# A gated-recurrence and mixture-of-experts layer on one core: the router in four column tiles, normalised rows turned by VectorE by way of DRAM, and the first expert's rows gathered whole

## The chip, the cores and the metric

The kernel runs on one core of a Trainium2 chip. The metric is the device time of one execution in microseconds; the time before is the median of three runs. A profile of one further execution goes with it. All arithmetic is in float32.

## The reference, cut to what matters

The input is 8 sequences of 1024 tokens with 512 features, 8192 tokens in all. Every token's row is normalised, and the normalised row feeds two branches whose product is added to the input.

```python
xn = layernorm(x)                                # (8192, 512)
# branch 1: a gated recurrence over each sequence
hidden, forget, inp = split(xn @ W1 + b1, 3)     # three times 1024 features
s = scan_over_time(hidden, forget, inp, init_h) @ W2 + b2
# branch 2: a shared expert, and one of 32 routed experts per token
shared = (silu(xn @ sgate) * (xn @ sup)) @ sdown # 1024 wide
logits = xn @ gate_w                             # (8192, 32)
e, top = argmax(logits), max(logits)
xs = xn * sigmoid(top)
routed = (silu(xs @ rgate[e]) * (xs @ rup[e])) @ rdown[e]
out = x + s * silu(shared + routed)
```

## The kernel before, in words

**Dense stage.** The tokens go in 16 chunks of 512, each of four tiles of 128 rows. For a chunk the kernel needs the normalised rows transposed: `xnT`, features on the partitions in four blocks k. From it come the recurrence's three projections and the shared expert's gate and up projections, as 20 jobs of 256 output features. The weights of a job are loaded as `nat`. From chunk 1 on, a job is done as Strassen's seven products (P1 to P7, L638), with sums of weight blocks (`sums`, kept in DRAM, L544) and differences of `xnT` blocks (`t`, "t sums", L570). ScalarE evicts each product, and VectorE or GpSimd joins them in pairs (L664); the tiles for P1's eviction, tag `p1`, have two buffers. Beside the jobs run the cell and gate arithmetic (reciprocal, sigmoid, scan, L702 to L784) and the second projections, the "fill" (L925), whose weights `wP` are fetched as each unit ends (L855, L858).

**The order.** In this stage the order of instructions is written out by hand. Time is counted in slots; a chunk has 140 of them (SC), and in each slot one product of two matmuls is issued. From chunk 1 on a slot lasts about 1.22 us. `at(slot, step)` places a step in a slot; each engine then does its instructions in the order in which they were issued, and waits for what they need. After the last chunk the slots go on with fill alone. Sync (SP) issues the plain DMAs and GpSimd (POOL) the indirect ones, each in its own order.

**Preparation of the next chunk.** `Prep.plan` places, in the slots of chunk c, what chunk c+1 needs (50 slots later in chunk 0): load of the rows, statistics, the power that gives 1/sigma (`spread`, on POOL), `normal` (L392), `transpose` on TensorE through PSUM with an eviction by ScalarE (L405, L408), the router's matmuls (L416), a transposition of the logits back to token rows (L426), the argmax (`choose`, L436 to L444), the score, and `scale`, which multiplies the normalised rows by the score and stores them to `rec1` (L453, L454). `rec2` holds x, the recurrence's output and the shared expert's output, for the experts' last step. The tiles x, `lgT` and the larger tiles of the table share a pool of five buffers.

**The table of tokens by expert.** `Dispatch` counts, for every token, its rank in its expert (`ranks`, every four chunks; two matmuls `bef`, L1000 and L1003, that need the running sums L989), then sorts the experts by size (`places`), gives each token a cell (`slots`), and writes token numbers by 64 scatters on POOL (`enter`, L1172) into eight tables, which are read back (`collect`) and merged (`merge`). `idx` holds the merged token numbers, and `fours` numbers of quarter rows, made from a copy of the table in DRAM (`numbers`, L1207). Numbers become available only at the passage to the experts.

**The experts.** Each of the 32 chunks has a fixed width, 376 tokens at most. `gather_in` (L199) fetches `xs` in pieces: each indirect DMA brings quarter rows of 32 tokens, so that VectorE's transposition of 32 by 32 blocks (L222) gives features on partitions. `gather_rest` (L210) fetches the rows of `rec2`; a VectorE addition (L272) waits for it. Then `compute` does gate, up and down products (L247, L236) with `h` from VectorE between (L255). In this stage the framework orders the instructions.

Of the kernel before, what the change touches and what calls it, by code (L numbers as in the profile page):

```python
# [33 lines left out]
def tile_kernel(  # L34
# [39 lines left out]

    nc = tc.nc
    B, S, H = x.shape
    N = B * S
# [86 lines left out]
    class Chunk:  # L166
# [3 lines left out]

        def __init__(self, alloc, alloc_w, name, cols, fours, width, w_src):
# [20 lines left out]
        def gather_in(self):  # L194
            self.xs = []
            for t, n in self.tiles:
                r = self.alloc([P, NA, HA], "xs", f"{self.name}_xs{t}")
                for b in range(-(-n // BL)):
                    nc.gpsimd.indirect_dma_start(  # L199
                        out=r[:, b, :], out_offset=None,  # L200
                        in_=rec1.rearrange("n (a d) -> (n a) d", a=NA),
                        in_offset=bass.IndirectOffsetOnAxis(ap=self.fours(t, b), axis=0),
                    )
                self.xs.append(r)

        def gather_rest(self):
            self.rest = []
# [8 lines left out]
        def transpose(self, t):  # L216
            if t >= len(self.tiles):
                return
            nb = -(-self.tiles[t][1] // BL)
            if t == 0:  # L220
                self.xsT = self.alloc([P, KH, C], "xsT", f"{self.name}_xsT")
            nc.vector.transpose(  # L222
                self.xsT[:, :, t * P : t * P + nb * BL].rearrange("p k (b c) -> p b k c", c=BL),
                self.xs[t][:, :nb, :].rearrange("p b (r k) -> p b k r", k=KH),
            )
# [72 lines left out]
    def alloc2(shape, tag, name):  # L298
# [3 lines left out]

    chunks = [
        Chunk(
            alloc2, alloc_w, f"e{e}", 
            lambda t, e=e: pools["idx"][:, e * CT + t : e * CT + t + 1],
            lambda t, b, e=e: pools["fours"][:, b, e * CT + t : e * CT + t + 1],
            WIDTHS[e], lambda e=e: expert(eid[0:1, e : e + 1]),
        )
        for e in range(E)  # L310
    ]
# [44 lines left out]
    class Prep:  # L356
# [37 lines left out]
                ALU.subtract, ALU.mult,  # L394
            )

        def transpose(self, t):
            if t == 0:
                xnTs[self.c] = jp.tile([P, KH, T], FP, tag="xnT", name=f"xnT{self.c}")
            if self.c or t > 1:  # L400
                tp = work(f"tp{self.c * NT + t}")
            else:
                tp = ps_x.tile([P, 512], FP, tag=f"x{t}", name=f"tp{t}")
            for k in range(KH):
                nc.tensor.transpose(  # L405
                    tp[:, k * P : (k + 1) * P], self.xs[t][:, k * P : (k + 1) * P], ident
                )
            nc.scalar.copy(  # L408
                xnTs[self.c][:, :, t * P : (t + 1) * P],
                tp.rearrange("p (k q) -> p k q", k=KH),  # L410
            )

        def router(self):
            lgp = work(f"lgp{self.c}")
            for k in range(KH):
                nc.tensor.matmul(  # L416
                    lgp[:E, :], lhsT=gw[:, k, :], rhs=xnTs[self.c][:, k, :],
                    start=(k == 0), stop=(k == KH - 1),
                )
            self.lgT = xp.tile([E, T], FP, tag="x", name=f"lgT{self.c}")  # L420
            nc.scalar.copy(self.lgT, lgp[:E, :])

        def logits(self):
            self.ps = work(f"lgt{self.c}")
            for t in range(NT):
                nc.tensor.transpose(  # L426
                    self.ps[:, t * E : (t + 1) * E], self.lgT[:, t * P : (t + 1) * P],
                    ident[:E, :E],
                )

        def choose(self):

            c = self.c
            lg = self.ps[:, : NT * E].rearrange("p (t e) -> p t e", t=NT)
# [60 lines left out]
    nc.sync.dma_start(out=gw, in_=gate_w.rearrange("(k p) e -> p k e", p=P))  # L495

    def zero_rows():
        for a in range(NA):
# [457 lines left out]
    class Dispatch:  # L956
# [16 lines left out]
        def ranks(self, q):  # L973
# [22 lines left out]
            yield  # L996
            yield
            yield
# [11 lines left out]
            )  # L1010
            yield
            nc.vector.tensor_reduce(rank[:, q : q + G], prev, AX.X, ALU.add)
            yield
            if q + G == NTILE:
                self.totals = work("cps")
                nc.tensor.matmul(
# [171 lines left out]
        def merge(self, which):  # L1188
            two = self.two
            if which < 2:  # L1190
                nc.vector.tensor_tensor(two[which], two[which], two[which + 2], ALU.min)
            elif which == 2:
                nc.vector.tensor_tensor(two[0], two[0], two[1], ALU.min)
            else:
                nc.vector.tensor_tensor(two[0][:, 0, :], two[0][:, 0, :], two[0][:, 1, :], ALU.min)
                self.table = dram.tile([P, NCOL], FP, name="table")
                nc.sync.dma_start(out=self.table[:, :], in_=two[0][:, 0, :])

        def numbers(self, half):

            if half == 0:
                nc.vector.tensor_copy(pools["idx"], self.two[0][:, 0, :])
# [47 lines left out]
    def spread_out(gen):  # L1250
        if next(gen, gen) is not gen:
            at(now + 1, spread_out, gen)

    at(SC + 90, d.clear)
    for q in range(NCHUNK // GC - 1):
        at(SC * (GC * (q + 1) - 2) + 80, lambda q=q: spread_out(d.ranks(q)))
    last = SC * (NCHUNK - 1)

    def table():
        for part in (d.ranks(NCHUNK // GC - 1), d.places(), d.slots()):  # L1260
            yield from part
        first = max(now + 3, last - 2)
        end = first + (12 * NTILE) // 5
        for i in range(NTILE):
            at(first + (12 * i) // 5, d.enter, i)
        at(end + 4, d.collect)
        for which in range(4):
            at(end + 13 + which, d.merge, which)
        for half in range(2):
            at(max(end + 20, END + 1) + half, d.numbers, half)  # L1270
# [159 lines left out]
```

## Time and profile before

| what | us |
|---|---|
| median of three runs | 4409.75 |
| lowest and highest | 4408.37, 4411.7 |
| the profiled execution | 4412.07 |
| its span, first to last instruction | 4410.3 |
| dense stage up to the last chunk's first product | 2654 |
| first product of the first expert, at | 2899 |

In the profile, PE is TensorE's matmuls and PEld its weight loads, DVE is VectorE, ACT is ScalarE, POOL is GpSimd, and SP is Sync; a q behind an engine's name is its queue of DMA issues. A row of groups gives line, engine, operation, output and inputs, shapes and count, then busy time and mean ns of one, then the idle time of the engine just before them, and who ended it. A row in order of time gives start, length, engine and line, and in brackets the wait ahead of it. A float32 matmul is two matmul instructions. A PE record runs to the end of its pipeline, so what a matmul costs TensorE is read from one start to the next.

### The profile page before, as it was taken

How to read it: one execution, taken by the hardware profiler on the slowest of the kernel's cores; microseconds unless marked ns; L12 is line 12 of the kernel's file. 1: busy time of each engine (PE TensorE's matmuls, PEld its weight loads, DVE VectorE, ACT ScalarE, POOL GpSimd, SP SyncE). 2: the span in 40 equal slices, each digit the busy share in tenths (PEclk: the TensorE clock that was granted, in tenths of full speed). 3: DMA queues.
4: the chain of work that ended last, by engine and by line, in shares of the span. 5: the costliest groups of instructions: out<-in, count | busy, mean ns of one | idle time of the engine just before them, and what ended most of it. 6: DMA issues, size and time to landing. Idle time of an engine off the chain costs nothing. (4 is left out here: it accounts for less than half of the span.)

```text
span 4410.3 us, 52402 instructions
## 1 busy us (share of the span) xinstructions
PE 4317.4 (98%) x19259; PEld 3586.4 (81%) x19259; DVE 2729.3 (62%) x3431; ACT 1709.4 (39%) x3379; POOL 1773.1 (40%) x1419
## 2 busy tenths in 40 slices
PE   8899999999999999999999999979999999999998
PEld 3488888888888888888888888846777788889997
DVE  6776876786977767877777698713333434443332
ACT  3355555555555555555555554401111111111111
POOL 4445343444444435444534456642233323332210
PEclk9999999999999999999999999989999999999999
DMA  7555655556556565555565555555455556565661
GB/s 239 186 185 185 202 186 196 179 196 208 177 188 204 187 195 184 193 202 177 195 202 188 194 172 177 179 202 177 174 195 209 181 180 226 183 236 197 216 227 63
DMA packets 408121, 842.39 MB, mean 191 GB/s; under 512 B 30060, under 2 KB 249868, under 8 KB 399669
## 3 DMA queue, kind: packets, MB, share of 16 engines
q1 hardware_dynamic: 380132, 749.01, 50.1%
q0 software_dynamic: 27728, 89.99, 6.4%
q8 instruction: 154, 2.52, 0.2%
q14 instruction: 107, 0.87, 0.1%
HBM read 756.20 MB, written 100.77 MB: 194 GB/s over the span
## 5 line engine op out<-in xcount | busy, mean ns | idle before, releaser
L638 PE MATMUL b<-t,sums 128*128 128x256 f32 x2400 | 617.1, 380 | 5.5 <-DVE t L570 3.9
L925 PE MATMUL u<-wP,s 128*128 128x256 f32 x2048 | 601.1, 380 | 2.7 <-DMA wP<-tdram 1.9
L236 PE MATMUL e_acc<-e_h,e_wd 128*128 128x296 f32 (+15 forms) x2048 | 515.4, 397 | 17.6 <-DVE e_h L255 17.5
L247 PE MATMUL e_g<-e_xsT,e_wg 128*128 128x296 f32 (+15 forms) x2048 | 520.4, 397 | 9.6 <-DVE e_xsT L222 8.2
L247 PE MATMUL e_u<-e_xsT,e_wu 128*128 128x296 f32 (+15 forms) x2048 | 518.0, 396 | 0.0
L638 PEld LDWEIGHTS b<-t,sums 128*128 128x128 f32 x2400 | 456.2, 190 | 70.7 <-issue 6.0
L199 POOL DMA_INDIRECT e_xs<-rec,fours x288 | 273.3, 949 | 561.2 <-DVE e_xsT L222 467.0
L236 PEld LDWEIGHTS e_acc<-e_h,e_wd 128*128 128x128 f32 x2048 | 389.9, 191 | 106.7 <-DVE e_h L255 19.1
L247 PEld LDWEIGHTS e_u<-e_xsT,e_wu 128*128 128x128 f32 x2048 | 389.0, 190 | 87.1
L247 PEld LDWEIGHTS e_g<-e_xsT,e_wg 128*128 128x128 f32 x2048 | 383.5, 191 | 91.6 <-DVE e_xsT L222 8.7
L925 PEld LDWEIGHTS u<-wP,s 128*128 128x128 f32 x2048 | 383.3, 190 | 64.3 <-issue 15.2
L722 DVE RECIPROCAL d<-d 128x512 f32<-128x512 f32 x128 | 428.0, 3345 | 1.6
L252 ACT ACTIVATE e_sig<-e_g 128x280 f32<-128x280 f32 (+15 forms) x256 | 102.6, 401 | 790.8 <-PE e_g L247 784.4
L254 DVE TENSOR_TENSOR e_sig<-e_sig,e_g 128x280 f32<-128x280 f32 (+15 forms) x256 | 112.1, 438 | 420.1 <-ACT e_sig L252 420.0
L638 PE MATMUL c<-t,sums 128*128 128x256 f32 x1200 | 308.7, 380 | 5.0 <-issue 3.7
L706 POOL TENSOR_TENSOR f<-m,f 128x1024 f32<-128x1024 f32 x64 | 154.9, 2421 | 381.0 <-DVE m L702 381.0
L638 PE MATMUL a<-xnT,nat 128*128 128x256 f32 x1200 | 308.0, 379 | 0.0
L638 PE MATMUL b<-xnT,nat 128*128 128x256 f32 x1200 | 308.0, 379 | 0.0
L638 PE MATMUL b<-t,nat 128*128 128x256 f32 x1200 | 307.9, 379 | 0.0
L638 PE MATMUL c<-xnT,sums 128*128 128x256 f32 x1200 | 307.9, 379 | 0.0
L638 PEld LDWEIGHTS c<-t,sums 128*128 128x128 f32 x1200 | 227.9, 190 | 36.6 <-issue 4.1
L638 PEld LDWEIGHTS b<-xnT,nat 128*128 128x128 f32 x1200 | 228.0, 190 | 31.4 <-issue 0.5
(230 smaller groups left out, 7298.3 us busy)
## 6 DMA issues: line engine op xcount, KB each, us to landing
sums<-sdram SPq DMA_DIRECT2D x300, 512.0 KB, 4.2
nat<-in_L_attn_W_dram SPq DMA_DIRECT2D x192, 512.0 KB, 4.3
wP<-tdram SPq DMA_DIRECT2D x128, 512.0 KB, 3.9
e_wg<-L_ffn_routed_gate_w_dram SPq DMA_DIRECT2D x32, 2048.0 KB, 15.4
e_wu<-n_L_ffn_routed_up_w_dram SPq DMA_DIRECT2D x32, 2048.0 KB, 8.6
e_wd<-L_ffn_routed_down_w_dram SPq DMA_DIRECT2D x32, 2048.0 KB, 13.6
nat<-L_ffn_shared_gate_w_dram SPq DMA_DIRECT2D x64, 512.0 KB, 4.3
nat<-n_L_ffn_shared_up_w_dram SPq DMA_DIRECT2D x64, 512.0 KB, 3.5
```

The lines of the kernel that those rows point to most:

```text
L199: nc.gpsimd.indirect_dma_start(out=r[:, b, :], out_offset=None, in_=rec1.rearrange("n (a d) -> (n a) d", a=NA), in_offset=bass.IndirectOff ...
L236: nc.tensor.matmul(accs[m][:, :W], lhsT=wd[:, j, m * P : (m + 1) * P], rhs=h[:, :W], start=(j == 0), stop=(j == NI - 1),)
L247: nc.tensor.matmul(o[:, :W], lhsT=w[:, k, j * P : (j + 1) * P], rhs=xsT[:, k, :W], start=(k == 0), stop=(k == KH - 1),)
L252: nc.scalar.activation(sig[:, :W], g[:, :W], AF.Sigmoid)
L254: nc.vector.tensor_tensor(sig[:, :W], sig[:, :W], g[:, :W], ALU.mult)
L638: nc.tensor.matmul(ps, lhsT=lhs[:, k, :], rhs=rhs[:, k, :], start=(new and k == 0), stop=(k == KQ - 1),  skip_group_check=True,)
L706: nc.gpsimd.tensor_tensor(v, self.m, v, ALU.subtract)
L722: nc.vector.reciprocal(self.d[:, s, :], self.d[:, s, :])
L925: nc.tensor.matmul(ps[:, q, :], lhsT=lhs[:, q * P : (q + 1) * P], rhs=w[:, p, :],  start=(q == 0 and p == 0 and name in ("P1", "P2", "P5") ...
```

## The change

- The normalised rows of chunks 1 to 15 no longer go through TensorE. Each tile is stored to a DRAM buffer `xnd` (`store`), read back by four DMAs as 32-row pieces (`pieces`), and transposed by one VectorE instruction of 32 by 32 blocks (`turn`). For `scale` the rows are read once more (`again`). Steps from the router on move to later slots.
- Partition p of block k now holds feature 4p + k instead of 128k + p. The weights `nat` and the gate are loaded to match, and the remaining TensorE transposes (chunk 0, first expert) read every fourth element.
- The router's four matmuls no longer accumulate: each writes its own 32 columns of the array (`tile_position`) and its own 32 PSUM partitions. The four parts are transposed as 128 by 128, and `choose` adds them with a reduction on VectorE.
- The ranks start 14 slots later, with nine slots instead of three ahead of their matmuls and four instead of one after the reduction. The scatters are spaced 11/5 slots instead of 12/5.
- The first expert's rows are gathered whole, by three indirect DMAs with `idx` alone, ahead of `numbers`, and transposed by TensorE. `idx` is copied right after the last merge.

The diff, cut to its core:

```diff
+    xnd = dram.tile([N, H], FP, name="xnd")
...
             for t, n in self.tiles:
                 r = self.alloc([P, NA, HA], "xs", f"{self.name}_xs{t}")
+                self.xs.append(r)
+                if self.whole:
+                    nc.gpsimd.indirect_dma_start(
+                        out=r.rearrange("p a d -> p (a d)")[:n, :], out_offset=None,
+                        in_=rec1[:, :],
+                        in_offset=bass.IndirectOffsetOnAxis(ap=self.cols(t)[:n, :], axis=0),
+                    )
+                    continue
...
+            if self.whole:
+                ps = work(f"{self.name}_tp{t}")
+                rows = self.xs[t].rearrange("p a (q k) -> p (a q) k", k=KH)
+                for k in range(KH):
+                    nc.tensor.transpose(
+                        ps[:, k * P : k * P + n], rows[:n, :, k], ident[:n, :n]
+                    )
+                nc.vector.tensor_copy(
+                    self.xsT[:, :, t * P : t * P + n],
+                    ps.rearrange("p (k q) -> p k q", k=KH)[:, :, :n],
+                )
+                return
...
+        def store(self, t):
+            i = (self.c * NT + t) * P
+            nc.sync.dma_start(out=xnd[i : i + P, :], in_=self.xs[t])
+
+        def pieces(self, t):
+            i = (self.c * NT + t) * P
+            x = self.xs[t] = xp.tile([P, NA, H // NA], FP, tag="x", name=f"xq{self.c * NT + t}")
+            rows = xnd[i : i + P, :].rearrange("(b c) (a d) -> a c b d", c=BL, a=NA)
+            for a in range(NA):
+                nc.sync.dma_start(out=x[a * BL : (a + 1) * BL, :, :], in_=rows[a])
+
+        def turn(self, t):
...
+            nc.vector.transpose(
+                xnTs[self.c][:, :, t * P : (t + 1) * P].rearrange("p k (b c) -> p b k c", c=BL),
+                self.xs[t].rearrange("p b (r k) -> p b k r", k=KH),
+            )
+
+        def again(self, t):
+            i = (self.c * NT + t) * P
+            self.xs[t] = xp.tile([P, H], FP, tag="x", name=f"xr{self.c * NT + t}")
+            nc.sync.dma_start(out=self.xs[t], in_=xnd[i : i + P, :])
...
             for k in range(KH):
                 nc.tensor.matmul(
-                    lgp[:E, :], lhsT=gw[:, k, :], rhs=xnTs[self.c][:, k, :],
-                    start=(k == 0), stop=(k == KH - 1),
+                    lgp[k * E : (k + 1) * E, :], lhsT=gw[:, k, :], rhs=xnTs[self.c][:, k, :],
+                    start=True, stop=True, tile_position=(0, k * E),
                 )
...
-                at(g + 36 + 2 * t, self.normal, t)
-                at(g + 38 + 2 * t, self.transpose, t)
-                at(g + 70 + t, self.scale, t)
+                at(g + 32 + 2 * t, self.normal, t)
+                at(g + 35 + 2 * t, self.store, t)
+                at(g + 43 + 2 * t, self.pieces, t)
+                at(g + 50 + 2 * t, self.turn, t)
+                at(g + 72 + 2 * t, self.again, t)
+                at(g + 86 + t, self.scale, t)
...
-            at(g + 48, self.router)
-            at(g + 56, self.logits)
-            at(g + 60, self.choose)
-            at(g + 66, self.score)
+            at(g + 66, self.router)
+            at(g + 72, self.logits)
+            at(g + 76, self.choose)
+            at(g + 80, self.score)
...
-            out=w, in_=src[:, base : base + 2 * P].rearrange("(k p) f -> p k f", p=P)
+            out=w, in_=src[:, base : base + 2 * P].rearrange("(p k) f -> p k f", p=P)
...
-        at(max(end + 20, END + 1) + 5, chunks[0].gather_in)
-
-    at(last - SC + 80, lambda: spread_out(table()))
+    at(last - SC + 94, lambda: spread_out(table()))
```

More of the change, by code (lines that the diff above doesn't have):

```diff
@@ L166, in tile_kernel, with __init__ @@
     class Chunk:
-        def __init__(self, alloc, alloc_w, name, cols, fours, width, w_src):
+        def __init__(self, alloc, alloc_w, name, cols, fours, width, w_src, whole=False):
+            self.whole = whole
             self.alloc, self.alloc_w, self.name, self.w_src = alloc, alloc_w, name, w_src
@@ L203, in gather_in @@
                     )
-                self.xs.append(r)
         def gather_rest(self):
@@ L218, in transpose @@
                 return
-            nb = -(-self.tiles[t][1] // BL)
+            n = self.tiles[t][1]
+            nb = -(-n // BL)
             if t == 0:
                 self.xsT = self.alloc([P, KH, C], "xsT", f"{self.name}_xsT")
+            if self.whole:
[10 more added lines that the diff above has]
+                return
             nc.vector.transpose(
@@ L307, in tile_kernel @@
             lambda t, b, e=e: pools["fours"][:, b, e * CT + t : e * CT + t + 1],
-            WIDTHS[e], lambda e=e: expert(eid[0:1, e : e + 1]),
+            WIDTHS[e], lambda e=e: expert(eid[0:1, e : e + 1]), e == 0,
         )
@@ L395, in normal @@
             )
+        def store(self, t):
[8 more added lines that the diff above has]
+        def turn(self, t):
+            if t == 0:
+                xnTs[self.c] = jp.tile([P, KH, T], FP, tag="xnT", name=f"xnT{self.c}")
+            nc.vector.transpose(
[6 more added lines that the diff above has]
+            nc.sync.dma_start(out=self.xs[t], in_=xnd[i : i + P, :])
         def transpose(self, t):
@@ L399, in transpose @@
                 xnTs[self.c] = jp.tile([P, KH, T], FP, tag="xnT", name=f"xnT{self.c}")
-            if self.c or t > 1:
+            if t > 1:
                 tp = work(f"tp{self.c * NT + t}")
@@ L405, in transpose @@
                 nc.tensor.transpose(
-                    tp[:, k * P : (k + 1) * P], self.xs[t][:, k * P : (k + 1) * P], ident
+                    tp[:, k * P : (k + 1) * P], self.xs[t].rearrange("p (q k) -> p k q", k=KH)[:, k, :], ident
                 )
@@ L416, in router @@
                 nc.tensor.matmul(
-                    lgp[:E, :], lhsT=gw[:, k, :], rhs=xnTs[self.c][:, k, :],
-                    start=(k == 0), stop=(k == KH - 1),
-                )
-            self.lgT = xp.tile([E, T], FP, tag="x", name=f"lgT{self.c}")
-            nc.scalar.copy(self.lgT, lgp[:E, :])
+                    lgp[k * E : (k + 1) * E, :], lhsT=gw[:, k, :], rhs=xnTs[self.c][:, k, :],
+                    start=True, stop=True, tile_position=(0, k * E),
+                )
+            self.lgT = xp.tile([P, T], FP, tag="x", name=f"lgT{self.c}")
+            nc.scalar.copy(self.lgT, lgp)
         def logits(self):
@@ L426, in logits @@
                 nc.tensor.transpose(
-                    self.ps[:, t * E : (t + 1) * E], self.lgT[:, t * P : (t + 1) * P],
-                    ident[:E, :E],
+                    self.ps[:, t * P : (t + 1) * P], self.lgT[:, t * P : (t + 1) * P], ident
                 )
@@ L433, in choose @@
             c = self.c
-            lg = self.ps[:, : NT * E].rearrange("p (t e) -> p t e", t=NT)
+            lg = self.lgT[:, : NT * E].rearrange("p (t e) -> p t e", t=NT)
+            nc.vector.tensor_reduce(
+                lg, self.ps.rearrange("p (t k e) -> p t e k", t=NT, k=KH), AX.X, ALU.add
+            )
             self.top = top = sm.tile([P, NT], FP, tag="top", name=f"top{c}")
@@ L494, in tile_kernel @@
         load(n)
-    nc.sync.dma_start(out=gw, in_=gate_w.rearrange("(k p) e -> p k e", p=P))
+    nc.sync.dma_start(out=gw, in_=gate_w.rearrange("(p k) e -> p k e", p=P))
     def zero_rows():
@@ L995, in ranks @@
             nc.vector.tensor_tensor(self.run, prev[:, G - 1, :], oh[:, G - 1, :], ALU.add)
-            yield
-            yield
-            yield
+            for _ in range(9):
+                yield
             ps = work(f"bef{q}")
@@ L1012, in ranks @@
             nc.vector.tensor_reduce(rank[:, q : q + G], prev, AX.X, ALU.add)
-            yield
+            for _ in range(4):
+                yield
             if q + G == NTILE:
@@ L1195, in merge @@
                 nc.vector.tensor_tensor(two[0][:, 0, :], two[0][:, 0, :], two[0][:, 1, :], ALU.min)
+                nc.vector.tensor_copy(pools["idx"], self.two[0][:, 0, :])
                 self.table = dram.tile([P, NCOL], FP, name="table")
@@ L1199, in numbers @@
         def numbers(self, half):
-            if half == 0:
-                nc.vector.tensor_copy(pools["idx"], self.two[0][:, 0, :])
             f = self.big([P, 2, NCOL], f"number{half}")
@@ L1252, in spread_out @@
             at(now + 1, spread_out, gen)
-    at(SC + 90, d.clear)
+    at(SC + 100, d.clear)
     for q in range(NCHUNK // GC - 1):
-        at(SC * (GC * (q + 1) - 2) + 80, lambda q=q: spread_out(d.ranks(q)))
+        at(SC * (GC * (q + 1) - 2) + 94, lambda q=q: spread_out(d.ranks(q)))
     last = SC * (NCHUNK - 1)
@@ L1262, in table @@
         first = max(now + 3, last - 2)
-        end = first + (12 * NTILE) // 5
+        end = first + (11 * NTILE) // 5
         for i in range(NTILE):
-            at(first + (12 * i) // 5, d.enter, i)
+            at(first + (11 * i) // 5, d.enter, i)
         at(end + 4, d.collect)
@@ L1268, in table @@
             at(end + 13 + which, d.merge, which)
+        at(max(end + 17, END + 1), chunks[0].gather_in)
         for half in range(2):
-            at(max(end + 20, END + 1) + half, d.numbers, half)
-        at(max(end + 20, END + 1) + 5, chunks[0].gather_in)
-    at(last - SC + 80, lambda: spread_out(table()))
+            at(max(end + 20, END + 4) + half, d.numbers, half)
+    at(last - SC + 94, lambda: spread_out(table()))
     fill = project_out()
```

## The prediction

> **What bounds the kernel now.** I read the page's busy shares and slices first, then busy time by stage, the groups by shape, and last the order of time around the places that the change touches.
>
> ```profile
> PE 4317.4 (98%) x19259; PEld 3586.4 (81%) x19259; DVE 2729.3 (62%) x3431; ACT 1709.4 (39%) x3379; POOL 1773.1 (40%) x1419
> PE   8899999999999999999999999979999999999998
> DVE  6776876786977767877777698713333434443332
> ```
>
> TensorE (PE) is the bound almost everywhere; its slices dip at the start and at one place near 70%, the passage from the dense stage to the experts. VectorE (DVE) is a third idle. By stage:
>
> ```profile
> 560.00:740.00 180.00, 180.00 (x835) 155.63 (x834) 129.15 (x136) 97.15 (x192) 80.17 (x56) 1.00 0.59 195
> 1296.70:1346.70 50.00, 50.00 (x229) 41.17 (x228) 49.69 (x46) 27.89 (x56) 24.41 (x15) 1.00 0.52 160
> 1349.30:1360.90 11.60, 11.60 (x55) 10.23 (x54) 2.66 (x5) 7.76 (x15) 8.34 (x5) 1.00 0.76 271
> 2900.00:3000.00 100.00, 81.11 (x249) 48.39 (x249) 21.85 (x35) 7.78 (x16) 38.55 (x42) 0.90 0.52 179
> ```
>
> Columns after the times: PE, PEld, DVE, ACT, POOL busy, clock, DMA share, GB/s. In the dense stage PE never waits: 835 instructions in 180 us, 0.2156 us each. A chunk has 280 + 112 float32 matmuls of two instructions, 169.1 us; chunks measure 175.3 us, so some 6.1 us are preparation. Second and third row: inside a chunk (slots 41 to 80) DVE is full, then nearly idle for ten slots. Fourth: at the passage PE idles and its clock drops.
>
> ```profile
> L222 DVE STREAM_TRANSPOSE e_xsT<-e_xs 128x512 f32<-128x512 f32 x63 | 66.0, 1081 | 16.0 <-DMA e_xs<-rec,fours 16.0
> L405 PE MATMUL tp<-ident,x 128*128 128x128 f32 x256 | 41.0, 285 | 17.4 <-DVE x L392 16.8 <-ACT xnT L408 0.7
> L416 PE MATMUL lgp<-xnT,gw 128*32 128x512 f32 x128 | 57.9, 595 | 0.0
> ```
>
> ```profile
> 411.15 0.60 PE L405 MATMUL tp<-ident,x 128*128 128x128 f32 x4
> 411.59 0.60 PE L925 MATMUL u<-wP,s 128*128 128x256 f32 x2
> ...
> 424.56 1.03 PE L638 MATMUL c<-xnT,sums 128*128 128x256 f32 x4
> 425.52 3.62 PE L416 MATMUL lgp<-xnT,gw 128*32 128x512 f32 x8
> 429.07 0.70 PE L925 MATMUL u<-wP,s 128*128 128x256 f32 x2
> ```
>
> Costs on PE are from start to start: one tile's transposes take 411.59 - 411.15 = 0.44 us. The router's eight instructions are 0.429 apart (3.43), and with about 0.31 of gaps at its ends hold PE 3.75 us. The four logit transposes hold it 0.56 in the same way. Together 4 x 0.44 + 3.75 + 0.56 = 6.05 us, which is the 6.1 above.
>
> **The change, part by part.**
>
> *Transposes of x, chunks 2 to 15 (14 chunks).* All 1.74 us leave PE, and four evictions (0.59 each) leave ACT, which is not the bound. DVE takes four block transposes of 1.08 (the L222 row, same shape): 4.3 us. SP gains 4 stores, 16 piece loads and 4 reloads. Its issues last about 0.4 us in the trace, so 10 us per chunk; the 16 pieces fill some 6.5 of the 8.5 us between slots 43 and 50. SP waits mostly for PE to release buffers, and weights are asked for two jobs (14 slots, 17 us) ahead, so I cost these at nothing; without that cover PE would wait a few us per chunk. The pieces wait for a store to land (3.7 us for 256 KB, rec<-x) and stand 8 slots (9.8 us) behind theirs; next on SP are weight loads. POOL's queue gains nothing here. Three MB more per chunk on some 34 moves DMA from 0.59 to about 0.65.
>
> *Where DVE stands.* The transposes enter at slots 50 to 56, the full stretch. DVE also loses there the 5.5 us that PE no longer spends on transposes and router, gets 4.3 us of work, and loses one or two us as normal and scale move out. Lining joins (L664) up with the matmul count, the latest join now ends 10.9 us after its slot began, at slot 47, and PE does not wait; one near the table's work ends 14.7 us late. The p1 tiles (two buffers) allow 9 slots, 11 us, plus the time that an accumulation bank stays in reserve. I expect 12 to 14 us, hence little stall: 0.3 us per chunk (0 to 2). The router at slot 66 needs the last transpose by then; DVE should end it about 1.4 us earlier. The idle ten slots absorb the rest.
>
> *A rule on the port.* Two rows of one moment:
>
> ```profile
> 1127.57 3.37 DVE L726 TENSOR_TENSOR i<-i,d 128x1024 f32<-128x1024 f32 x1
> ```
> ```profile
> 1127.47 2.39 POOL L706 TENSOR_TENSOR f<-m,f 128x1024 f32<-128x1024 f32 x1 [8.52 <-DVE m L702]
> ```
>
> The same product runs in 1.22 us undisturbed. The Trainium skill, "SBUF — State Buffer", section "SBUF: two separate sides", says that VectorE and GpSimd lock a shared port, the loser waiting a whole instruction, and names VectorE work with two SBUF inputs or in a two-port mode. A block transpose has one input; by the row 1.08 us holds, while if it took the lock too, each would wait up to 2.4 us more, 10 us per chunk. No row shows one beside a POOL product. I take 1.08.
>
> *Router.* No row has column tiles. Above nothing: 3.75 if they do not overlap. Below: two instruction times plus gaps, 0.86 + 0.31 = 1.17. "TensorE: Matmul & The Clock Gate", "Measured speedup vs the span model", gives 2.38x for three column tiles, which would make about 1.4 + 0.31 = 1.7; section "The mechanism" says that matmuls start in program order. A float32 matmul here is two instructions on one tile, and the second cannot overlap the first: a1, then a2 with b1, and so on, five times 0.429 + 0.31 = 2.46. I take 2.46, saving 1.29 (0 to 2.6).
>
> *Logits.* Four 128-wide transposes at 0.44 for 0.56: 0.12 saved. The sum over k adds one DVE reduction of 512 per partition, near the 0.68 of rank's, at slot 76.
>
> Sum per chunk: 1.74 + 1.29 + 0.12 - 0.3 = 2.85; times 14, 39.9 us. The first router: 1.3.
>
> *Chunk 1's preparation, inside chunk 0.* PE now waits 9.9 us at 116.4 for normalised rows. That wait goes; DVE's lag stays, and next late are the stores, behind which SP holds weight loads. Bounds -5 and +12; I take 6, since DVE idles 12 us later in this chunk, part of which it can win back.
>
> *Room in the ranks.* Before their second matmul PE waits 0.9 us in three of four (DVE prev L989): 2.7 saved. The table work moves about 20 slots, onto the t sums of chunk 15, where PE already loses 3.9 + 0.7 us. It has less backlog then, but more work beside it: 0 (-6 to +4).
>
> *Edits at no cost.* Weights and gate are read with rows 4p to 4p+3 in partition p: pieces of 1 KB for the weights as before, at the same issue. The first chunk's transposes read every fourth element; if that halved their speed, 16 x 0.11 = 1.8 us would show at the start.
>
> *First expert's rows.*
>
> ```profile
> 2876.82 1.00 POOL L199 DMA_INDIRECT e_xs<-rec,fours  x1 [14.77 <-DVE fours L1207]
> ...
> 2930.49 0.94 POOL L210 DMA_INDIRECT e_rest<-rec,idx  x1 [0.30 <-issue]
> ```
> ```profile
> 2898.98 4.64 PE L247 MATMUL e_g<-e_xsT,e_wg 128*128 128x376 f32 x8 [8.25 <-DVE e_xsT L222]
> ...
> 2945.79 2.87 PE L236 MATMUL e_acc<-e_h,e_wd 128*128 128x376 f32 x4 [17.54 <-DVE e_h L255]
> ```
>
> Twelve gathers of 1.25 us become three, issued after the index copy (2864) instead of the numbers (2877). The expert's start: the 8.25 us become twelve transposes at 0.11 and a copy, some 2.5, and the slow first group (4.64 for 2.69) goes. But the 17.54 behind it is set by e_rest, whose gathers stand on POOL behind all xs gathers; a DVE add waits for them, and h behind that. With e1's gathers starting near 2880 instead of 2894, e_rest and so PE resume about 13 us earlier. I take 13 (0, if the order behind changes, to 26, if both waits vanish).
>
> Total: 39.9 + 1.3 + 2.7 + 6 + 13 = 62.9. The profiled execution took 4412.07 (span 4410.3 and 1.8 around it), 2.3 above the median: 4349.2, so **4347** on the median's scale.
>
> **The rivals.**
> - *Column tiles overlap fully.* For it: a page's speedups; against: two instructions per tile. 15 x 1.29 = 19 less: 4328.
> - *They do not overlap.* No row of column tiles speaks for them. 19 more: 4366.
> - *VectorE becomes the bound in slots 41 to 80 (slower).* If transposes wait for the port, lateness reaches some 23 us against about 15 that buffers bear: 8 us of PE stall per chunk, against 3.15 saved. 14 x 4.85 = 68, less 23 elsewhere: 4410 + 45 = 4455. It decides from 4.8 us of stall per chunk up, where 67 us eat the 67 that all parts would bring without any. Against: one input, and DVE's later idle time.
> - *The passage keeps its wait:* 4360.
>
> **How the numbers follow.** Main case (4347, itself 4325 to 4370 with the passage's and chunk 0's bounds) 0.50; full overlap 0.22; none 0.15; stalls that eat most of the gain 0.06, of which 0.04 leave no change; slower 0.07. Range 4312 to 4390: below, full overlap with half of the passage's and chunk 0's further room; above, no overlap with no gain at the passage and some stall. The bound of "same" is 0.2%, 8.8 us, about what a measurement of this kernel tells. Faster 0.89, same 0.04, slower 0.07.
>
> **What would show it.** Chunks of about 172.4 us in the PE timeline; no L405 rows after chunk 0; 60 block transposes near 1.08 on DVE; the eight lgp instructions within 1.7 us from first to last start (3.0 now); e_rest gathers near 2917 less what the dense stage gained. I am wrong if PE shows waits for DVE xnT or p1 tiles in each chunk, or if block transposes show 2 to 3 us.

## The result, and the profile after

The changed kernel takes 4344.32 us (median of 4 runs, 4343.11 to 4346.68) beside 4409.39 for the kernel before in the same session: ratio 0.9852, 95% interval 0.9835 to 0.9869. Forecast were 4347 and a range of 4312 to 4390. The total is right, but by luck: of its terms several are wrong, in both directions, and their errors cancel.

First the page's busy shares and slices of the changed kernel, then busy time by stage (PE, PEld, DVE, ACT, POOL, then clock, DMA share, GB/s). The stages answer to those shown of before, moved by what the chunks ahead have gained; the last is the first 100 us of the experts.

```profile
PE 4262.1 (98%) x19031; PEld 3560.0 (82%) x19031; DVE 2761.5 (64%) x3507; ACT 1661.3 (38%) x3319; POOL 1748.4 (40%) x1410
PE   8899999999999999999999999999999999999998
DVE  6787877886977778778878788723334334343332
```
```profile
560.00:740.00 180.00, 179.98 (x838) 157.01 (x837) 133.64 (x143) 96.56 (x192) 83.22 (x59) 1.00 0.66 211
1271.00:1320.00 49.00, 48.98 (x232) 41.67 (x231) 48.79 (x42) 26.65 (x53) 22.46 (x16) 1.00 0.74 236
1322.00:1333.60 11.60, 11.60 (x56) 10.21 (x55) 6.31 (x11) 7.54 (x16) 8.00 (x4) 1.00 0.57 176
2860.00:2960.00 100.00, 94.48 (x307) 58.34 (x306) 29.07 (x48) 9.46 (x19) 30.49 (x31) 0.97 0.53 184
```

The dip of PE's slices at 70% is gone. In the steady stretch (560 to 740 us) PE still never waits; VectorE stays full in the stretch of slots 41 to 80, and a part of its work has moved into the ten slots behind it (6.31 us busy where there were 2.66). The DMA share rose from 0.59 to 0.66, as expected. By groups with their shapes:

```profile
L436 DVE STREAM_TRANSPOSE xnT<-xq 128x512 f32<-128x512 f32 x60 | 63.8, 1096 | 0.0
L467 PE MATMUL lgp<-xnT,gw 128*32 128x512 f32 x128 | 17.0, 604 | 3.7 <-DVE xnT L436 3.7
L485 DVE TENSOR_REDUCE lgT<-lgt 128x128 f32<-128x512 f32 x16 | 10.9, 679 | 8.5 <-PE lgt L477 8.5
```

The block transposes take 1.096 us on average, and only one router (in chunk 0) waited for them, 3.7 us. The router's busy time fell from 57.9 to 17.0 us, although each of its 128 instructions lasts as long as before (604 ns, 595 then): they lie on top of each other. Order of time on PE in one chunk, the router between two products:

```profile
1128.77 1.03 PE L694 MATMUL b<-t,sums 128*128 128x256 f32 x4
1129.73 1.06 PE L467 MATMUL lgp<-xnT,gw 128*32 128x512 f32 x8
1130.73 0.70 PE L981 MATMUL u<-wP,sh 128*128 128x256 f32 x2
```

From its first start to the next instruction the router holds PE 1.00 us, where it was 3.55 (425.52 to 429.07); with the 0.2 us of gaps at its ends, 1.20 instead of 3.75.

Where the time of the profiled execution went (span 4343.3 instead of 4410.3), by the first product of each chunk and stage:

| stretch | before | after | difference |
|---|---|---|---|
| chunk 0, with what lies ahead | 185.65 | 179.20 | -6.46 |
| chunk 1 | 178.01 | 180.72 | +2.70 |
| chunks 2 to 13 (most 175.28, then 171.2 to 171.6) | | | -49.72 |
| chunk 14 | 179.77 | 183.89 | +4.12 |
| chunk 15 to its last product | 187.32 | 187.91 | +0.59 |
| fill behind it | 48.80 | 52.70 | +3.90 |
| last fill product to first expert's first | 8.63 | 2.79 | -5.84 |
| first expert | 84.62 | 69.51 | -15.11 |
| all others | | | -1.2 |

So there are also losses. First the wait for normalised rows in chunk 0 of before, then the longest waits of after, on PE in order of time (two in chunk 0, the start of chunk 1, chunk 14, the start of chunk 15):

```profile
126.78 1.09 PE L405 MATMUL tp<-ident,x 128*128 128x128 f32 x4 [9.78 <-DVE x L392]
```
```profile
124.73 2.07 PE L654 MATMUL b<-xnT,nat 128*128 128x512 f32 x2 [4.96 <-ACT u L661]
...
152.79 1.06 PE L467 MATMUL lgp<-xnT,gw 128*32 128x512 f32 x8 [3.71 <-DVE xnT L436]
186.66 2.07 PE L694 MATMUL c<-t,sums 128*128 128x256 f32 x4 [6.43 <-DVE t L626]
...
2582.05 0.76 PE L1131 MATMUL terms<-terms,ones 32*128 32x129 f32 x2 [6.49 <-DVE terms L1127]
2620.48 1.10 PE L694 MATMUL b<-t,sums 128*128 128x256 f32 x4 [3.79 <-DVE t L626]
```

In all but the first VectorE is late. That first one was hidden before, behind the wait for rows: the evictions stand on ACT behind an instruction that waits for a product of GpSimd (4.22 us, POOL i L762). Before, the waits at the start of chunk 1 made 4.6 us (1.26, 2.11 and 1.22) and now make 9.0 (6.43, 0.53 and 2.02), and chunk 14 had none longer than 0.73.

A long wait can cost more than its row says, since TensorE's clock drops behind it. In the stretch behind the 6.43 us, and in the one behind the wait for `terms`, the granted clock (the column behind POOL) was 0.50 and 0.81:

```profile
186.50:190.00 3.50, 3.34 (x8) 2.69 (x9) 3.50 (x5) 1.14 (x3) 0.69 (x1) 0.50 0.04 15
2582.00:2597.00 15.00, 14.95 (x58) 12.47 (x59) 7.82 (x14) 5.40 (x11) 0.72 (x1) 0.81 0.31 101
```

At the passage to the experts, POOL's gathers and PE:

```profile
2814.62 1.00 POOL L205 DMA_INDIRECT e_xs<-rec,idx  x1 [1.35 <-DVE idx L1252]
...
2832.33 0.98 POOL L212 DMA_INDIRECT e_xs<-rec,fours  x1 [14.13 <-DVE fours L1262]
...
2856.02 0.95 POOL L222 DMA_INDIRECT e_rest<-rec,idx  x1 [0.30 <-issue]
```
```profile
2848.26 2.79 PE L272 MATMUL e_g<-e_xsT,e_wg 128*128 128x376 f32 x8 [0.98 <-DVE e_xsT L242]
2871.74 5.38 PE L261 MATMUL e_acc<-e_h,e_wd 128*128 128x376 f32 x8 [5.52 <-DVE e_h L280]
```

The first expert's rows are on their way 18 us before the first quarter-row numbers are to be had. The wait of 8.25 us is 0.98, that of 17.54 is 5.52.

### The profile page after: what moved, and what is told of

Its sections match the earlier page's. It is cut to its first block, busy times and chain, and to the rows that moved or that the text cites. A ratio compares the mean times of both kernels' runs of the same rounds, so it can differ in the third digit from the quotient of the medians.

```text
span 4343.3 us, 52479 instructions
## 1 busy us (share of the span) xinstructions
PE 4262.1 (98%) x19031; PEld 3560.0 (82%) x19031; DVE 2761.5 (64%) x3507; ACT 1661.3 (38%) x3319; POOL 1748.4 (40%) x1410
## 5 line engine op out<-in xcount | busy, mean ns | idle before, releaser
L212 POOL DMA_INDIRECT e_xs<-rec,fours x276 | 263.1, 953 | 553.3 <-DVE e_xsT L247 458.7
L762 POOL TENSOR_TENSOR f<-m,f 128x1024 f32<-128x1024 f32 x64 | 154.8, 2419 | 410.6 <-DVE m L758 321.7
L694 PEld LDWEIGHTS c<-xnT,sums 128*128 128x128 f32 x1200 | 227.1, 190 | 37.1 <-ACT p L708 6.3
```

Of the source, the lines that this page charges most:

```text
L212: nc.gpsimd.indirect_dma_start(out=r[:, b, :], out_offset=None, in_=rec1.rearrange("n (a d) -> (n a) d", a=NA), in_offset=bass.IndirectOff ...
L694: nc.tensor.matmul(ps, lhsT=lhs[:, k, :], rhs=rhs[:, k, :], start=(new and k == 0), stop=(k == KQ - 1),  skip_group_check=True,)
L762: nc.gpsimd.tensor_tensor(v, self.m, v, ALU.subtract)
```

## The experiments

They ran in a later session on two chips, where the kernel before took 4431 us (medians of 4431.67, 4430.87 and 4431.45), 22 more than in the first. So each is set against the changed kernel of that session, which ran on one of the two chips, and the dense stage is read from the traces, where equal steady chunks agree within 0.1 us.

**The changed kernel again.**

> The changed kernel itself, unaltered, beside the experiments on one chip. Two executions of the dense stage have agreed to 0.1 us a chunk so far, while the passage to the experts has differed by 8 us between kernels that have the same instructions there. If the passage is a matter of the execution and not of the kernel, this run shows another time between the last fill product and the second expert's first product than the 72.3 us of the first profile (70 to 82). If it shows 72 again, the edits of the first experiments shifted the passage.

4357.71 us, ratio to before 0.9836 (0.9819 to 0.9852): the same gain within the interval. The dense stage was the same (chunks 2 to 13 within 0.02 us; chunk 1 took 1.7 more). From the last fill product to the second expert's first it took 80.5 us instead of 72.3. So the passage is a matter of the execution too; differences below some 8 us in a total are read here from the stretch that was edited.

**Router without column tiles.**

```diff
-lgp[k * E : (k + 1) * E, :], ..., start=True, stop=True, tile_position=(0, k * E)
+lgp[:E, :], ..., start=(k == 0), stop=(k == KH - 1)
```

> The changed kernel, with one part undone: the router's four float32 products accumulate again in one set of 32 PSUM partitions (no column tiles), and the logits are transposed as 32 by 128 with no reduction over k. Theory A (the four column tiles overlap entirely, router 3.75 us without them and 1.19 with, in 16 chunks): 2.55 x 16 = 41 us back on TensorE, less some 2 us where TensorE waits anyway, so about 4344 + 39 = 4383. Theory B (the two instructions of each product serialise with the neighbour tile, saving 1.29 per chunk, and the rest of the gain in a chunk comes from elsewhere): + 19, about 4363. If the column tiles brought nothing: 4344. In the trace the eight starts of lgp should again lie 3.0 us apart.

4394.20 us, 36.5 above the changed kernel. A steady chunk takes 173.88 instead of 171.21: 2.67 us, which is 2.55 of the router and 0.12 of the logit transposes. Theory A holds.

```profile
972.75 3.62 PE L467 MATMUL lgp<-xnT,gw 128*32 128x512 f32 x8
976.30 0.70 PE L979 MATMUL u<-wP,sh 128*128 128x256 f32 x2
```

**Two column tiles.**

```diff
-lgp[k * E : (k + 1) * E, :], ..., start=True, stop=True, tile_position=(0, k * E)
+lgp[k // 2 * E : (k // 2 + 1) * E, :], ..., start=(k % 2 == 0), stop=(k % 2 == 1),
+    tile_position=(0, k // 2 * E)
```

> The changed kernel with the router in two column tiles instead of four: k = 0 and 1 accumulate in the first, k = 2 and 3 in the second, issued in this order. It asks how the tiles share the array. Independent tiles that start whenever their own columns are free, whatever was issued ahead: 4 x 0.429 + 0.31 = 2.03 us from first start to next instruction. Whole products started in program order (the second tile's first waits for the first tile's second): 6 x 0.429 + 0.31 = 2.9. Single instructions started in order: 7 x 0.429 + 0.31 = 3.3. Against the changed kernel's 1.19 a steady chunk grows by 0.84, 1.7 or 2.1 us, the kernel by 13, 26 or 33.

4369.38 us, 11.7 more; most steady chunks 172.20, 1.0 more.

```profile
962.24 1.92 PE L467 MATMUL lgp<-xnT,gw 128*32 128x512 f32 x8
964.09 0.70 PE L983 MATMUL u<-wP,sh 128*128 128x256 f32 x2
```

1.85 us from start to start, 2.05 with the gaps: independent tiles. The starts of the eight instructions in the three traces, in us from the first:

```
four tiles  0.000 0.007 0.014 0.020  0.454 0.460 0.467 0.474
two tiles   0.000 0.013  0.453 0.466  0.882 0.896  1.311 1.325
one set     0.000 0.453 0.882 1.311 1.741 2.170 2.599 3.028
```

With two tiles, the third product (first of the second tile) starts 13 ns behind the first, ahead of the first's second instruction and of the second product, though the kernel's text issues it third. (The records don't name the tile; that each pair is one of each tile follows from two instructions of one tile never being less than 0.42 us apart.)

**Transposes on TensorE in all chunks.**

```diff
-at(g + 35 + 2 * t, self.store, t)
-at(g + 43 + 2 * t, self.pieces, t)
-at(g + 50 + 2 * t, self.turn, t)
-at(g + 72 + 2 * t, self.again, t)
+at(g + 38 + 2 * t, self.transpose, t)
```

> The changed kernel, with another part undone: in all chunks TensorE transposes the normalised rows by way of PSUM as before (in the slots of before), with no store to DRAM, no pieces read back, no block transposes on VectorE and no second read for the scale. Column tiles, ranks and the passage stay as changed. Theory A (the transposes cost TensorE 0.44 us a tile and the replacement on VectorE and the queues costs steady chunks nearly nothing): + 1.74 x 13 = 23 us in chunks 2 to 14, less what chunks 0 and 1 win back (they lost 5 us to VectorE's lateness in the changed kernel), so about 4344 + 18 = 4362, 4355 to 4369. Theory B (VectorE's 4.3 us more per chunk eat part of it): under + 10. In chunk 1 a wait for sums at its start (6.4 us now) should be gone by A's account of the loss.

4371.63 us, 13.9 more; steady chunks 172.73, 1.52 more of the 1.74 that the transposes hold PE. The detour by DRAM and VectorE costs PE some 0.2 us a chunk: theory A. The wait at chunk 1's start was not gone: it fell from 6.4 to 3.2 us and the next one rose from 0.5 to 2.9, so that the three there make 6.5 us of the 9.0. What remains above the 4.6 of before is not due to the block transposes.

**Block transposes done twice.**

```diff
+for _ in range(2):
     nc.vector.transpose(xnTs[self.c]..., self.xs[t]...)
```

> The changed kernel with each block transpose of VectorE done twice into the same place: 4.4 us more of VectorE per chunk in its fullest stretch, nothing else. Theory A (VectorE's lateness has room: by its later idle slots and the buffers ahead of TensorE): the steady chunks stay within 0.5 us of 171.2, chunk 0 and 1 lose some 4 each, the kernel + 5 to + 15. Theory B (the changed kernel stands already at the edge of what the buffers bear): a wait of TensorE for joins or for xnT of about 4 us in each chunk, + 60.

4430.59 us, 72.9 more, and level with the kernel before (ratio 0.9998, 0.9989 to 1.0007). Theory B: of 4.4 us more on VectorE at least 3.5 reach PE (steady chunks of 174.7 instead of 171.2), and in chunks 2 to 13 it is 4.6 on average. The chain in one chunk, on VectorE, ACT and PE:

```profile
975.92 6.63 DVE L437 STREAM_TRANSPOSE xnT<-xq 128x512 f32<-128x512 f32 x6
...
995.18 1.22 DVE L793 SCALAR_TENSOR_TENSOR h<-m,h 128x1024 f32<-128x1024 f32 x1
```
```profile
996.43 1.06 ACT L834 ACTIVATE ssig<-g 128x1024 f32<-128x1024 f32 x1 [7.79 <-DVE h L793]
997.39 0.46 ACT L711 ACTIVATE u<-b,vec 128x256 f32<-128x256 f32 x1
```
```profile
997.90 1.13 PE L695 MATMUL b<-t,sums 128*128 128x256 f32 x4 [3.19 <-ACT u L711]
```

A sigmoid (`ssig`) waits on ACT for VectorE's `h`; the evictions of PSUM stand behind it in ACT's queue, and PE waits for one of them (`u`). In the changed kernel the same instruction waits too, but PE doesn't:

```profile
965.81 1.06 ACT L833 ACTIVATE ssig<-g 128x1024 f32<-128x1024 f32 x1 [4.33 <-DVE h L792]
```

Between 4.33 and 7.79 us of that wait PE's reserve ends: 4.4 us of VectorE work cost 3.5, so under 1 us was free.

In each chunk from 2 to 13 PE's long wait is this one of 3.19 us. Yet four of them take 177.6 to 178.0 us, and chunk 9 takes 176.45. In these the clock dropped behind the wait: in chunk 4 PE's next thirteen instructions came 0.43 us apart instead of 0.216. The stretch behind the wait in chunk 4 (177.57 us) and in chunk 5 (174.75 us), with clocks of 0.80 and 1.00:

```profile
820.00:835.00 15.00, 14.62 (x55) 12.42 (x56) 12.98 (x20) 6.03 (x16) 3.92 (x3) 0.80 0.52 182
997.00:1012.00 15.00, 14.10 (x65) 12.45 (x66) 13.16 (x19) 7.66 (x20) 3.42 (x2) 1.00 0.57 203
```

So the same wait cost 3.5 us or 6.4; what decides which is not shown.

**First expert's rows in pieces.**

```diff
-    WIDTHS[e], lambda e=e: expert(eid[0:1, e : e + 1]), e == 0,
+    WIDTHS[e], lambda e=e: expert(eid[0:1, e : e + 1]), False,
-at(max(end + 17, END + 1), chunks[0].gather_in)
...
+at(max(end + 20, END + 4) + 5, chunks[0].gather_in)
```

> The changed kernel, with the first expert's rows gathered in pieces of 32 tokens again, with quarter row numbers and after these have been made, and transposed by VectorE. Theory A (the passage's gain comes from the three gathers with idx, issued ahead of the numbers, and from POOL being free the sooner for the second expert's and the rest's gathers): the waits of some 8 us ahead of the first expert's gate products and of 17 ahead of its down products return; + 21, less up to 4 that the end of the dense stage loses now, so about 4363, 4360 to 4366. Theory B (the gain at the passage comes mostly from scatters and merges that end earlier, by their closer spacing): + 8 at most, and the first gather of the pieces would start near 2820 rather than 2828.

4372.97 us, 15.3 more, though its four runs lie 16 us apart (4363.47 to 4379.84). In the trace, from the last fill product to the second expert's first it took 90.4 us, 9.9 more than the changed kernel there. Both waits return, and the first gather of the pieces starts at 2833, no sooner than the first gather of pieces in the changed kernel, so the closer scatters are not the cause:

```profile
2852.64 5.38 PE L272 MATMUL e_g<-e_xsT,e_wg 128*128 128x376 f32 x8 [7.60 <-DVE e_xsT L247]
2882.75 2.88 PE L261 MATMUL e_acc<-e_h,e_wd 128*128 128x376 f32 x4 [16.74 <-issue]
```

**TensorE for chunk 1's rows alone.**

```diff
+if self.c == 1:
+    at(g + 38 + 2 * t, self.transpose, t)
+    continue
 at(g + 35 + 2 * t, self.store, t)
```

> The changed kernel, with TensorE transposing chunk 1's rows alone (the first preparation that runs beside chunk 0); all others go by DRAM and VectorE. Theory A (in chunk 0 and at the start of chunk 1 TensorE waits for VectorE, 3.7 us at the router for the last block transpose, 6.4 and 2.0 for the t sums and later, because VectorE takes 4.3 us more and takes it late): the waits at chunk 1's start shrink, - 3 to - 5 us, about 4340. Theory B (the waits come from GpSimd's long cell products ahead of the sums, and would be there at any rate): the transposes' 1.74 us come back on TensorE and nothing goes, 4344 to 4347; and if the wait for normalised rows of before returns with them (9.9 us), up to 4352.

4355.78 us, 1.9 less, too little to tell from the total. In the trace chunk 1's end comes 4.4 us sooner than in the repeated run of the changed kernel (356.88 instead of 361.24; 3.0 sooner than in its first), as theory A has it. But the three waits at chunk 1's start still make 6.6 us (4.6 before), which theory A does not explain; what causes them was not tried. The wait for rows comes back only in part, 3.9 us where it was 9.8 before, and most of what is won is given back in chunks 14 and 15 and the fill.

```profile
118.07 1.10 PE L455 MATMUL tp<-ident,x 128*128 128x128 f32 x4 [3.88 <-DVE x L417]
126.61 0.75 PE L455 MATMUL tp<-ident,x 128*128 128x128 f32 x4 [2.34 <-ACT xnT L458]
183.64 1.13 PE L697 MATMUL c<-t,sums 128*128 128x256 f32 x4 [3.12 <-DVE t L629]
```

**Old spacing inside the ranks.**

```diff
-            for _ in range(9):
+            for _ in range(3):
                 yield
             ps = work(f"bef{q}")
...
             nc.vector.tensor_reduce(rank[:, q : q + G], prev, AX.X, ALU.add)
-            for _ in range(4):
-                yield
+            yield
```

> The changed kernel with the old spacing inside the ranks (three slots instead of nine ahead of the first bef matmul, none more after the reduction), which still start 14 slots later; places and slots of the table follow nine slots sooner. Theory A (the spacing is what took the 0.9 us wait of each rank chunk away, each rank chunk having gained 1.0 us more than its neighbours): rank chunks 6, 10 and so on go from 172.9 back to 173.8, + 2.7 in all, less what the table wins by starting sooner in chunk 14. Theory B (the later start alone did it): they stay at 172.9. In chunk 14 the wait for terms (6.7 us) is not touched by this: 6 to 7 there, or less if the tables' work lies better nine slots sooner.

4365.42 us, 7.7 more. A rank chunk takes 174.69 instead of 172.92, the chunk behind it 0.37 less: 1.4 net each, so the spacing, not the later start, took the wait away. In chunk 14 the wait for `terms` was gone, but ranks and t sums waited in its place, and up to the last product chunks 14 and 15 lost 4.3 more:

```profile
2555.72 1.12 PE L1058 MATMUL bef<-prev,ones 128*128 128x512 f32 x2 [1.48 <-DVE prev L1045]
2564.33 0.41 PE L1071 MATMUL cps<-run,ones 128*128 128x32 f32 x2 [2.74 <-DVE prev L1063]
...
2629.15 1.19 PE L694 MATMUL b<-t,sums 128*128 128x256 f32 x2 [4.38 <-DVE t L626]
```

**Three edits.** TensorE for chunk 1's rows as above, and

```diff
 nc.vector.tensor_copy(terms[:, 4 * E :], extra)
-            for _ in range(4):
+            for _ in range(10):
                 yield
...
-            nc.vector.tensor_tensor(r[:n, H : 2 * H], r[:n, H : 2 * H], b2b[:n, :], ALU.add)
+            if not self.whole:
+                nc.vector.tensor_tensor(r[:n, H : 2 * H], r[:n, H : 2 * H], b2b[:n, :], ALU.add)
...
+            if self.whole:
+                zb = alloc([P, H], "s", f"{name}_zb{t}")
+                nc.vector.tensor_tensor(zb[:n, :], z[:n, :], b2b[:n, :], ALU.mult)
             nc.vector.tensor_tensor(z[:n, :], z[:n, :], r[:n, H : 2 * H], ALU.mult)
+            if self.whole:
+                nc.vector.tensor_tensor(z[:n, :], z[:n, :], zb[:n, :], ALU.add)
```

> Three small edits to the changed kernel: TensorE transposes chunk 1's rows; ten slots instead of four lie ahead of the matmul that sums the places' terms; and the first expert adds the bias of the recurrence's output only after its product with the gate, so that no VectorE instruction that waits for the gathered rest can stand ahead of the expert's h. Theory (each wait is what its row names): - 3 in chunks 0 and 1, - 4 to - 6 in chunk 14 (the wait of 6.5 us for terms), - 5 at the first down products, together 10 to 14 under the changed kernel on the same chip. Rival (the waits pass on: later terms make the scatters and so the tables later, and the passage grows by as much): 3 to 5 under it.

4341.03 us, 16.7 less than the changed kernel, more than expected and otherwise divided: 4.4 up to the end of chunk 1, 12.5 in chunks 14 and 15 (175.03 and 183.31 instead of 182.97 and 187.91), a net 1 at the passage, and 1.6 lost again in the fill. In chunks 14 and 15 the edit of chunk 1 alone (above) won nothing, so this is the six slots. The wait for `terms` (6.5 us) is gone, the waits behind it shrank from 7.1 to 4.2 us, and the remaining 3 us fit the clock: it stayed at 1.00 in the 15 us from the `terms` product on, where in the changed kernel it was 0.88. The third edit failed: VectorE's order put transposes of the second expert's rows ahead of the first expert's `h`, and these waited in place of the addition.

```profile
2840.28 1.11 DVE L247 STREAM_TRANSPOSE e_xsT<-e_xs 128x512 f32<-128x512 f32 x1 [8.24 <-DMA e_xs<-rec,fours]
...
2845.59 0.55 DVE L280 TENSOR_TENSOR e_h<-e_sig,e_u 128x376 f32<-128x376 f32 x1
```

**And the second expert's rows gathered whole.**

```diff
-    WIDTHS[e], lambda e=e: expert(eid[0:1, e : e + 1]), e == 0,
+    WIDTHS[e], lambda e=e: expert(eid[0:1, e : e + 1]), e < 2,
 at(max(end + 17, END + 1), chunks[0].gather_in)
+at(max(end + 17, END + 1), chunks[1].gather_in)
```

> The three edits (TensorE for chunk 1's rows, ten slots ahead of the terms matmul, the first experts' bias added after the gate product) and a fourth: the second expert's rows too are gathered whole with idx, right behind the first expert's, and transposed by TensorE. In the run of the three edits the first expert's h stood on VectorE behind transposes of the second expert's rows (8.2 us of wait for e_xs), and the gathers of the rest on POOL behind eleven piece gathers of 1.25 us. Theory: both go, the passage from the last fill product to the second expert's first falls from 79.5 us to 70 to 73 (58.1 of it the first expert's own products as in the second, and some 7 of transposes and of low clock), at a price of 1.3 us of TensorE: 4332 to 4336 on that chip. Rival (what holds the passage there is the waits that no row names, up to 15 us ahead of sigmoids and h): no change, 4339 to 4343.

4324.55 us (4322.84 to 4325.06): 33.2 less than the changed kernel there, ratio to before 0.976 (0.9743 to 0.9776). From the last fill product to the second expert's first it takes 65.0 us instead of 79.5, more gain than the theory had (70 to 73). No wait of PE at the passage is left but one of 1 us:

```profile
2832.24 2.79 PE L272 MATMUL e_g<-e_xsT,e_wg 128*128 128x376 f32 x8 [0.99 <-DVE e_xsT L242]
2834.87 2.69 PE L272 MATMUL e_u<-e_xsT,e_wu 128*128 128x376 f32 x8
...
2842.45 2.69 PE L261 MATMUL e_acc<-e_h,e_wd 128*128 128x376 f32 x8
```

This version beats both kernels. Which of its parts freed the first `h` (the piece gathers gone from POOL, or the transposes from VectorE's order) was not tried apart.

## Why the prediction was right, and which of its steps failed

| step of the sum | forecast gain | measured gain |
|---|---|---|
| 14 preparations at 2.85 | 39.9 | 57.0 (14 x 4.07) |
| first router | 1.3 | 2.7 |
| chunk 1's preparation, inside chunk 0 | 6 | -3.0 |
| room in the ranks | 2.7 | 1.2 |
| table's work moved | 0 | -12.7 |
| first expert's rows | 13 | 20.9 |
| other stretches | 0 | 0.9 |
| sum | 62.9 | 67.0 |

The measured column is the table of stretches, divided. A steady chunk (4, 5, 8, 9, 12) gained 4.07 us (175.28 to 171.21), and this is counted for all of chunks 1 to 14. What chunks 0 and 1 gained or lost besides stands in the rows for the first router and chunk 1; what the rank chunks (2, 6, 10) and those behind them gained besides, in the row for the ranks. The row for the table takes all that chunk 14, chunk 15 and the fill lost; of it 8.2 are chunk 14's, while the 3.9 of the fill are not shown to come from the table.

- *Router.* The step that failed is "a1, then a2 with b1, and so on, five times 0.429 + 0.31". The traces show all four tiles starting within 20 ns and their second instructions together 0.45 us later: two instruction times, 1.20 us with the gaps, saving 2.55 where 1.29 was taken. It was the lower bound of 1.17 that held, and with it the rival of full overlap, whose 19 us the forecast lacked. Had the other terms been right, the time would have been that rival's 4328. That matmuls start in program order, which the Trainium skill states in "TensorE: Matmul & The Clock Gate", section "The mechanism", was the reason for the wrong step. As it was applied here, product by product in the order of the kernel's text, the run with two tiles contradicts it; whether the array or an earlier step sets the order that the records show wasn't told apart. The page's 2.38 times is for three tiles; four gave 3.55 / 1.00 here.
- *Transposes off TensorE.* Right: 1.74 taken, 1.52 measured net by undoing it; 0.3 of stall forecast, 0.2 to 0.3 found. In steady chunks PE never waits for SP's queue, the stores or the pieces.
- *Where VectorE stands.* The latest join of a steady chunk now ends 12.9 us after its slot began, inside the forecast 12 to 14, and PE does not wait. That some 15 us is what the kernel bears was near too: with the transposes doubled the latest joins end at 14.2 to 14.6, and PE waits 3.2 us in each chunk. But what runs out first is not the two p1 tiles; it is ACT's queue behind the sigmoid that waits for `h`.
- *The port.* Right to let the row stand: the 60 block transposes took 1.096 us on average and 1.21 at most, and 57 of them ran beside GpSimd's products, where the shared lock would have made it 2 to 3. GpSimd's products of 128x1024 beside them were not longer either (2.38 us in 14 cases, 2.47 in the other 50). The slower rival needed 4.8 us of stall per chunk to eat the gain. Doubled transposes cost 4.6 a chunk by work alone, and gave the kernel before's time. The rival's mechanism was absent, but its threshold is near.
- *Chunk 1's preparation.* A gain of 6 was taken and 3.0 lost. "That wait goes" held (9.8 us), but 5.0 of it came back at the next wait, for ACT behind GpSimd. "DVE idles 12 us later in this chunk, part of which it can win back" failed: the late transposes held the router 3.7 us, and the lag went into the t sums of chunk 1, with a lower clock behind them. Undoing this part alone brought back 3.0 to 4.4 us.
- *Room in the ranks.* The spacing does take the wait away: without it a rank chunk takes 1.4 us more. But the chunk behind now takes 0.4 more than a steady one, so that of 2.7 us 1.2 are left.
- *Table.* "It has less backlog then, but more work beside it: 0 (-6 to +4)" failed, beyond its own bound. The step named the t sums of chunk 15, whose waits stayed as they were; the new wait was for `terms` in chunk 14, four slots behind a chain of small VectorE instructions, and the clock dropped behind it. Six slots more took it away and 12.5 us with it.
- *First expert's rows.* The mechanism held (three early gathers, POOL free sooner); the size is open. In the first two profiles the gain was 20.9 us: `e_rest` came 30 us sooner on the dense stage's scale (2930.49 to 2856.02, less the 45 of the dense stage and fill) where 13 were forecast. The two waits shrank by 7.3 and 12.0 us, and what lies between them by some 1.6. But this passage differs by 8 us between executions, and undoing the part brought back 9.9 us in the trace and 15.3 in the medians. The forecast 13 lies among these.

The terms that were taken too small (preparations, first router, first expert's rows) make 26 us, those that were taken too large (chunk 1's preparation, ranks, table) 23. This is why the profiled execution is only 4 us off the forecast, and the median 3.

## What to carry to other kernels

Cost each part of a change at its own place, then undo the parts one by one: here a total within 0.1% hid three terms that were wrong by 9 to 17 us, and a fourth whose size is open. When work moves to an engine that is a third idle, ask how late that engine may be and which in-order queue makes the lateness felt. The first 4.4 us a chunk cost 0.2 here, the next 4.4 cost 3.5, and 6.4 where the clock dropped too. So a wait on the engine that bounds the kernel is to be counted with the clock behind it. And where a moved step waits on a chain of small instructions (the terms, the ranks), slots between producer and consumer are worth more than the step's own place.

## What the runs showed of the hardware that was not expected

- Float32 products of 32 columns in separate column tiles run side by side entirely: eight instructions of 0.429 us in 1.00 us with four tiles, 1.85 with two, 3.55 with one. In the records the tiles proceed independently of the order in which the kernel's text issues their products; where that order is changed was not told apart.
- Behind a wait of 3.19 us TensorE's granted clock dropped to 0.80 over 15 us in one chunk and stayed at 1.00 in the next; the wait of 6.43 us was followed by 0.50 over 3.5 us.
- The first execution of the changed kernel and its repetition differ by 8 us at the passage. There ACT's and VectorE's instructions stand still for up to 15 us with no releaser in the trace, as ACT's first two sigmoids in the repeated run:

```profile
2861.22 0.48 ACT L277 ACTIVATE e_sig<-e_g 128x376 f32<-128x376 f32 x1 [15.33 <-remote]
2874.61 0.48 ACT L277 ACTIVATE e_sig<-e_g 128x376 f32<-128x376 f32 x1 [12.90 <-remote]
```

  The cause stays open. The DMA share there is about 1.0 (2846 to 2876 us), but so it is in the first execution (2845 to 2875 us), and the trace has no transfer on the queues of instructions from 2847 to 2875 us, so that it gives no sign of code being loaded then. Why the kernel before took 22 us more in the second session stays open as well: its trace there wasn't taken. The changed kernel lost 13 between the sessions, 8 of them at this passage and 4 in experts 16 to 29.
